# A graph layer with eight experts: the first two lots of tokens picked by one-hot products, and the parts without edges made in two PSUM banks

## The chip, the core and the metric

The kernel runs on one core of a Trainium2 chip. The metric is the device time of one execution in microseconds (us); the kernel before has a median of 1637.05 us over 5 runs (1624.28 to 1647.42). The engines are TensorE (PE, matrix products), VectorE (DVE), ScalarE (ACT), GpSimd (POOL, which here does nothing but issue indirect transfers) and SyncE (SP, which issues plain transfers). Each engine works through its own list of instructions in order and waits for the others by semaphores.

## The reference, cut to what matters

3125 nodes with 256 features, 100,000 edges sorted by their target node:

```python
xn = _layernorm(x, axis=-1)
x = x + gnn(xn, src, dst) + mix(xn)          # 3125 x 256
x = x + ffn(_layernorm(x, axis=-1))          # 8 experts, the 2 best of each token

# gnn: maximum over the edges that end in a node, 0 for a node without edges
e = relu((xn[dst] - xn[src]) @ theta.T + theta_b + xn[src] @ phi.T + phi_b)
out = segment_max(e, dst)

# ffn: a token goes to the two experts with the best logits
h = gelu(xe[e] @ W1[e] + b1[e])              # 256 -> 1024
y = h @ W2[e] + b2[e]                        # 1024 -> 256
out = sum over the two of weight * y
```

`mix` is a linear attention without softmax; it comes down to one 256x256 matrix that every node is multiplied by.

## The kernel before

**Tiles and groups.** The nodes lie in 25 tiles of 128. Since the edge gather is the longest work, the tiles are cut into five groups by the edges that end in them: group 0 is tiles 17 to 24, group 1 tiles 10 to 16, group 2 tiles 4 to 9, group 3 tiles 1 to 3, group 4 tile 0. The edges are gathered in 727 steps of 128 rows (`gather`, L127 to L130), 134 for group 0, 151 for group 1, 185 for group 2, 158 and 99 for the others. Each gathered row is folded into a running maximum on DVE (`fold`, L411 to L415). Eight gathers fill one of five windows (`wide`, pool of 5); a window is stored to DRAM by SP (`s_d`) and is then free. The largest targets, the first 16 nodes, have too many edges for that, and get their maxima in another way (`first_maxima`, L1206 on): it turns rows of a table by products with the identity (L1238), makes masks on PE (L1256) and takes maxima on DVE (L1222). It borrows one of the five windows for the rows that it turns.

**Parts without edges.** `without_edges` (L454 to L464) makes for each tile what doesn't depend on its edges: one row of biases (L452), two products of 128x512 (L459), and x itself through the identity (L460), all added up in one PSUM bank of 512 columns; two copies on ACT (L463, L464) bring it back. A class `Early` (L1385) gives it the bank: the tile named `trf`, of which there is one. `mixers` starts the 25 parts in order of the groups, 3.5 ticks apart in group 0 and 4.25 after that.

**Tokens.** When a group's edges are folded, `group` (L1424) starts `token_tile` for each of its tiles: the node's maximum is put together, x is updated, normalized into `xn2(i)`, and the router's logits and the two best experts are found. `dispatch` (L1397) then waits for the tiles of half a group, and `slots` (L589) counts for each expert which token comes where.

**Lots.** A lot is one expert with one group, 24 of them with 256 places (groups 0 to 2) and 8 with 128 (group 3). There are two ways to bring the tokens of a lot together:
- Groups 0 and 1: `dispatch` scatters each tile's rows to their places in DRAM (`xs_d`, two indirect transfers per tile, 8 for each half of group 0), ACT's queue loads the rows of two lots at a time (`rows`, L807), and `turn` (L848) transposes them on PE.
- Groups 2 and 3, called on chip (`on_chip`, L796): `hots` (L815 to L826) compares, for each tile of the group, the place numbers with the place that each token has for this expert, which gives a one-hot matrix for each tile; `turn` (L837) multiplies tile by one-hot and adds up over the tiles. That needs no transfer.

Both leave the turned lot in `trf`, and `scaled` (L859) puts it on ACT into `xe` with the expert's scale. Then `Units.run` makes 8 steps of the first product (L730) with a gelu each (L732), and the second product (L754) of a lot lies between the steps of the next one. `Stream.go` (L895 to L964) leads this: it prepares lot u+1 during lot u (`between`, L941 to L945): in step 1 it makes the one-hots of lot u+1 if that lot is on chip, and otherwise, if u is even, loads the rows of the next pair of lots. If the next lot is not prepared, the branch at L916 does it one after the other: load or one-hots, 8 ticks, turn, 2 ticks, scale, 2 ticks.

**What sets the order.** The order of instructions on PE, DVE, ACT and SP is written out by the program itself. Generators (`start`, L1350) yield a number of ticks until their next piece is due, and `tick` (L1354) runs what is due; each indirect transfer that POOL issues is one tick. Counted from the yields: the parts start at tick 180; the last of them, of tile 0, starts at 276. The scatter of the first half of group 0 comes at 258 and moves the clock to 266, that of the second half at 279 and moves it to 287. The ranks of the second half are known at 261. Group 0's lots are added to the list at 287. Lot 0 begins at 297, after load, turn and scale; lot 1 at 302, lot 2 at 317. `first_maxima` begins at 287 and its first transposes (L1238) stand at 293.

Of the kernel before, what the change touches and what calls it, by code (L numbers as in the profile page):

```python
# [19 lines left out]
P = 128  # L20
# [49 lines left out]
SPILL = 128  # L70
APART_3 = 32
# [9 lines left out]
def gps_layer(ctx: ExitStack, tc: tile.TileContext, x, src, dst, thetaT, phiT, biases, wq, wkvT,  # L81
# [507 lines left out]
    def slots(ro, ps, g, half, i0, i1, pick, taken, chosen=None):  # L589
# [38 lines left out]
        if chosen is not None:  # L628
            nc.vector.scalar_tensor_tensor(chosen[:, i0 - first:i1 - first, :], rank, 1.0, took, op0=OP.add, op1=OP.mult)
            clock["chosen", g, half] = True  # L630
            yield 1
# [29 lines left out]
        if chosen is not None:  # L661
            return
# [46 lines left out]
    class Units:  # L709
# [12 lines left out]
        def run(self, e, w1t, xe, w2t, done, between, parts, part):  # L722


            n = parts * part
            hT = []
            for f in range(FC):
                hp = self.ps.tile([P, ROWS], F32, name="hp")
                for c in range(2):
                    nc.tensor.matmul(hp[:, 0:n], w1t[:, c, f, :], xe[:, c, 0:n], start=(c == 0), stop=(c == 1))  # L730
                hT.append(self.hidden())
                nc.scalar.activation(hT[f][:, 0:n], hp[:, 0:n], AF.Gelu, bias=sm[:, 4 + f, e:e + 1])  # L732
                on_pe(n / P * 0.43)
# [33 lines left out]
    class Stream:  # L767


        def __init__(self, wts, act, ps):  # L770
            self.wts, self.act, self.ps = wts, act, ps
            self.lots, self.through, self.open = [], set(), True
            self.held = {}
            self.chosen = {}
            self.parts = []
            self.plan()
# [19 lines left out]
        def on_chip(self, u):  # L796
            return u < len(self.lots) and self.lots[u][0] >= G - 3
# [9 lines left out]
        def rows(self, v):  # L807
            if 2 * v < len(self.lots) and ("xs", v) not in self.held and not self.on_chip(2 * v):
                xs = self.held["xs", v] = self.at(v % 2)
                asked.append((self.lots[2 * v][0], move(nc.scalar, xs.rearrange("p (k s) d -> p k s d", k=2), self.two(v))))  # L810
                for g, put in sent:
                    if g > asked[-1][0]:
                        apart_in_rows(asked[-1][1], put)

        def hots(self, u):  # L815

            if self.on_chip(u) and ("hot", u) not in self.held:
                g, e = self.lots[u]
                n, nt = CAPS[g], GROUPS[g][1] - GROUPS[g][0]
                if g == G - 3:  # L820
                    flat = xn_hi[:, 7:13, :].rearrange("p s d -> p (s d)")
                else:
                    flat = xn_lo[:, 6:9, :].rearrange("p s d -> p (s d)")[:, u % 2 * nt * n:(u % 2 + 1) * nt * n]
                hot = self.held["hot", u] = flat.rearrange("p (i n) -> p i n", n=n)
                for i in range(nt):
                    nc.vector.tensor_scalar(hot[:, i, :], place_of[g], self.chosen[g][:, i, e:e + 1], None, op0=OP.is_equal)  # L826

        def turn(self, u):
            if ("hot", u) in self.held and ("tr", u) not in self.held:
# [12 lines left out]
                on_pe(1.5 if more is None else 6.1)  # L842
# [52 lines left out]
        def go(self):  # L895
# [5 lines left out]
            while True:  # L901
                if u == len(self.lots):
# [12 lines left out]
                    nc.scalar.activation(table, eps, AF.Gelu)  # L915
                if ("xe", u) not in self.held:  # L916
                    self.rows(u // 2)
# [467 lines left out]
    class Early:  # L1385

        def tile(self, shape, dt, name):
            return at_hand["ffp"].tile([P, 2, ROWS], dt, name="trf", bufs=1).rearrange("p c n -> p (c n)")
# [8 lines left out]
    def dispatch(g, half, i0, i1, top, top_i, taken):  # L1397
# [13 lines left out]
        yield from slots(ro, mm, g, half, i0, i1, made[0], taken)  # L1411
# [12 lines left out]
    def group(g):  # L1424
# [11 lines left out]
        if g >= G - 3 and g < G - 1:  # L1436
# [37 lines left out]
        if g < G - 2:  # L1474
            yield 5 if g < G - 3 else 0.5
            at_hand["ffn"].add(g)
# [163 lines left out]
    def mixers():  # L1640
# [195 lines left out]
```

## Time and profile before

| | us |
|---|---|
| median of 5 runs | 1637.05 |
| the profiled execution: its time, its span | 1623.73, 1621.9 |
| PE busy; weight load | 981.3; 736.7 |
| DVE busy | 794.9 |
| ACT busy | 331.9 |
| POOL busy | 837.1 |
| last gather of group 0's, group 1's, group 2's edges ends | 299.5, 584.1, 977.2 |
| last gather of all edges ends | 1448.1 |
| first gelu of group 0's, group 1's, group 2's lots | 597.4, 843.7, 1147.5 |

Mean granted TensorE clock: 0.788. In the rows of a timeline the columns are the start and the duration in us, engine, line, operation, output and input with partitions and elements, the number of merged instructions, and in brackets the idle time of the engine before it with what ended it. "issue" means that nothing seen in the profile was waited for, "remote" that what was waited for is not seen. The end of a matrix product is modelled, so a product can be done later than its row says. In the table of stretches the columns are the stretch, its length, and the busy time and number of instructions of PE, the weight load, DVE, ACT and POOL, then the granted clock, the DMA engines' busy share and the GB/s.

### The profile page before, as it was taken

The numbers are of one execution on the slowest core, as the hardware profiler recorded it, in microseconds if no ns is written. First come the engines' busy times: TensorE is split into PE (matmuls) and PEld (weight loads), VectorE is DVE, ScalarE is ACT, GpSimd is POOL, SyncE is SP. The second block draws the span as 40 slices with busy tenths as digits, with TensorE's granted clock in tenths as the row PEclk, the third lists the DMA queues.
The fourth block names the chain that finished last, engine by engine and source line by source line (L and its number), as shares of the span: only waits on it lengthen the run. The fifth ranks groups of instructions, "written<-read, shape, count | busy, mean of one in ns | idle before, by whom it ended". The sixth has DMA issues, their size and how long they took to land.

```text
span 1621.9 us, 14777 instructions
## 1 busy us (share of the span) xinstructions
PE 981.3 (61%) x4461; PEld 736.7 (45%) x4461; DVE 794.9 (49%) x2543; ACT 331.9 (20%) x799; POOL 837.1 (52%) x868
## 2 busy tenths in 40 slices
PE   3505775823528437648656777624787747679657
PEld 3402332412315126537535666513575535569547
DVE  4546974745318315437246566337566524424423
ACT  2301222300103012213112222102211103123212
POOL 6274465566564754554645544654555473642341
PEclk7756997966758768769868888756899977979869
DMA  7442564658436545657546786435476744647453
GB/s 234 137 127 84 195 223 141 208 181 316 168 91 227 183 127 182 204 170 244 186 139 193 263 275 208 156 110 204 130 255 206 259 136 156 228 158 276 139 170 134
DMA packets 100263, 300.96 MB, mean 186 GB/s; under 512 B 20099, under 2 KB 43002, under 8 KB 89550
## 3 DMA queue, kind: packets, MB, share of 16 engines
q0 software_dynamic: 41824, 113.70, 23.5%
q1 hardware_dynamic: 29180, 109.58, 17.5%
q10 hardware_dynamic: 29170, 76.65, 14.4%
q8 instruction: 37, 0.61, 0.1%
q14 instruction: 52, 0.43, 0.1%
HBM read 181.72 MB, written 118.13 MB: 185 GB/s over the span
## 4 chain that ended last, share of the span: by engine, by line
PE 36%; another core or an unknown queue 31%; DVE 14%; issue 12%; ACT 4%; DMA 2%; POOL 0%; ACTq 0%; SPq 0%; DVEq 0%; POOLq 0%
PE hp L730 13%; PE yp L754 9%; DVE g L414 4%; PE trf L837 3%; PE v L1291 2%; ACT ring L732 2%; PE k L1291 1%; PE trf L459 1%; PE mm L1256 1%; PE dots_p L1314 1%; DVE xn_hi L1222 1%; DVE tiles L1199 1%; PE mm L507 1%; DVE hit L343 1%
## 5 line engine op out<-in xcount | busy, mean ns | idle before, releaser
L129 POOL DMA_INDIRECT g<-b_d,srcI x727 | 706.1, 971 | 529.6 <-issue 238.7
L414 DVE SCALAR_TENSOR_TENSOR g<-g,cut 128x256 f32<-128x256 f32 x722 | 348.4, 483 | 60.7 <-DMA g<-b_d,srcI 25.2
L732 ACT ACTIVATE ring<-hp,sm 128x256 f32<-128x256 f32 (+1 forms) x320 | 137.1, 432 | 584.2 <-remote 242.4
L1222 DVE CUSTOM_DVE_ANT_0 xn_hi<-bT,mm 128x512 bf16<-128x512 f32 (+1 forms) x224 | 140.5, 627 | 211.0 <-remote 84.7
L730 PE MATMUL hp<-xe,big 128*128 128x256 f32 (+1 forms) x736 | 182.5, 374 | 97.8 <-ACT ring L732 68.5
L754 PE MATMUL yp<-big,ring 128*128 128x256 f32 x608 | 178.8, 416 | 11.8 <-ACT ring L732 5.3
L730 PEld LDWEIGHTS hp<-xe,big 128*128 128x128 f32 x736 | 129.3, 203 | 123.7 <-ACT ring L732 74.0
L730 PE MATMUL hp<-xe,w 128*128 128x256 f32 (+1 forms) x448 | 120.3, 405 | 103.5 <-issue 51.6
L730 PEld LDWEIGHTS hp<-xe,w 128*128 128x128 f32 x448 | 87.8, 227 | 122.5 <-issue 56.0
L754 PEld LDWEIGHTS yp<-big,ring 128*128 128x128 f32 x608 | 122.0, 213 | 30.8 <-ACT ring L732 5.7
L754 PE MATMUL yp<-w,ring 128*128 128x256 f32 x368 | 101.6, 398 | 0.0
L129 POOL DMA_INDIRECT r<-s_d,end_i x25 | 23.9, 958 | 115.6 <-DMA s_d<-g 41.2
L754 PEld LDWEIGHTS yp<-w,ring 128*128 128x128 f32 x368 | 71.5, 202 | 10.8
L1256 PE MATMUL mm<-ident_h,absent 128*128 128x128 bf16 x400 | 43.0, 234 | 41.0 <-issue 23.6
L129 POOL DMA_INDIRECT g<-ys_d,from_i x42 | 39.9, 949 | 40.1 <-DVE g L1577 21.8
L1300 DVE TENSOR_REDUCE var<-big 128x16 f32<-128x1024 f32 x25 | 30.4, 1216 | 61.3 <-ACT big L1297 55.6
L452 PE MATMUL trf<-thirds,which_bias 74*128 74x512 bf16 x25 | 11.6, 464 | 78.7 <-ACT x_sb L464 57.3
L1256 PEld LDWEIGHTS <-absent 128*128 128x128 bf16 x400 | 31.1, 105 | 57.2 <-issue 29.1
L1291 PE MATMUL v<-wkv,xn_hi 128*128 128x512 f32 x56 | 31.1, 682 | 36.9 <-ACT big L1296 32.1
L511 DVE TENSOR_SCALAR none<-mm 128x1 f32<-128x1 f32 x25 | 3.8, 153 | 97.2 <-remote 46.8
L837 PE MATMUL trf<-xn_hi,xn_lo 128*128 128x256 f32 x192 | 46.3, 393 | 3.7 <-DVE g L414 3.7
L563 DVE MAX8 top<-mm 128x8 f32<-128x8 f32 x25 | 4.3, 171 | 85.3 <-remote 58.7
(327 smaller groups left out, 1400.5 us busy)
## 6 DMA issues: line engine op xcount, KB each, us to landing
s_d<-g SPq DMA_DIRECT2D x75, 1024.0 KB
big<-in_w ACTq DMA_DIRECT2D x44, 512.0 KB
w<-in_w ACTq DMA_DIRECT2D x32, 512.0 KB
s_d<-g SPq DMA_DIRECT2D x13, 896.0 KB
g<-b_d,srcI POOLq DMA_INDIRECT x727
big<-in_w ACTq DMA_DIRECT2D x4, 2048.0 KB
ys_d<-ys ACTq DMA_DIRECT2D x24, 256.0 KB
xs_d<-zero ACTq DMA_DIRECT2D x16, 256.0 KB
```

What stands on the lines that cost most here:

```text
L129: got = nc.gpsimd.indirect_dma_start(out=to, out_offset=None, in_=table, in_offset=row_index(index))
L343: nc.vector.tensor_scalar(hit, keys[i], node[:, i:i + 1], 0.0, op0=OP.is_ge, op1=OP.add, accum_out=upto[:, i:i + 1])
L414: nc.vector.scalar_tensor_tensor(g[:, j, :], last, cut[:, t:t + 1], g[:, j, :], op0=OP.add, op1=OP.max)
L459: nc.tensor.matmul(am, xnT(i, c), am_w[:, c, :], start=False, stop=False)
L730: nc.tensor.matmul(hp[:, 0:n], w1t[:, c, f, :], xe[:, c, 0:n], start=(c == 0), stop=(c == 1))
L732: nc.scalar.activation(hT[f][:, 0:n], hp[:, 0:n], AF.Gelu, bias=sm[:, 4 + f, e:e + 1])
L754: nc.tensor.matmul(yp[r][0:part, :], hT[q][:, r * part:(r + 1) * part], w2t[:, q, :], start=(q == 0), stop=(q == FC - 1 and self.whole))
L837: nc.tensor.matmul(tr[:, c, 0:CAPS[g]], xn2(i)[:, c * P:(c + 1) * P], hot[:, i - i0, :], start=(i == i0), stop=(i == i1 - 1 and more is No ...
L1222: nc.vector.tensor_tensor_reduce(unread[:, 0:n * P], bT[:, h, 0:n * P], mask_p[:, 0:n * P], 1.0, NEG, op0=OP.add, op1=OP.max, accum_out=mo ...
L1256: nc.tensor.matmul(mask_p[:, i * P:(i + 1) * P], absent[:, at:at + 1].to_broadcast([P, P]), ident_h, start=True, stop=True)
L1291: nc.tensor.matmul(to, xnT(i, c), wkv[:, c, k * INNER:(k + 1) * INNER], start=(c == 0), stop=(c == 1))
L1300: nc.vector.tensor_reduce(var, sq, AX.X, OP.add)
```

## The change

It has three parts.
- A constant `AT_FIRST = 2`: the first two lots of group 0 count as on chip. Their one-hots (8 tiles of 128x256) lie in the first eight of the 14 slots of `ring`, both lots' in the same place, and their place numbers are those of group 2. For that `slots` keeps the ranks of group 0 in `chosen`, as for the later groups. Group 0's lots are added as soon as both halves have their ranks, and `go` makes lots 0 and 1 ready one after the other before lot 0 begins: one-hots, 2.5 ticks, turn, 5.5 ticks, scale, 1 tick. The scatters of group 0 stay as they are.
- A set `sent` of the groups whose scatters have been issued: rows are loaded for a lot only when its group is in it.
- The parts without edges use the two tiles named `hp` in place of the one named `trf`, so `hp` is declared with 512 columns (it took a bank of its own before as well), and they all start 3.25 ticks apart. 3 ticks after the last, `clock["parts"]` is set, for which `go` waits.

```diff
+AT_FIRST = 2
...
-        if chosen is not None:
+        if g >= G - 3:
             return
...
-                hp = self.ps.tile([P, ROWS], F32, name="hp")
+                hp = self.ps.tile([P, 2 * ROWS], F32, name="hp")
...
         def on_chip(self, u):
-            return u < len(self.lots) and self.lots[u][0] >= G - 3
+            return u < len(self.lots) and (self.lots[u][0] >= G - 3 or u < AT_FIRST)
...
         def rows(self, v):
-            if 2 * v < len(self.lots) and ("xs", v) not in self.held and not self.on_chip(2 * v):
+            if 2 * v < len(self.lots) and ("xs", v) not in self.held and self.lots[2 * v][0] in self.sent and not self.on_chip(2 * v):
...
-                if g == G - 3:
+                if g < G - 3:
+                    flat = ring[:, 0:nt, :].rearrange("p s d -> p (s d)")
+                elif g == G - 3:
...
-                    nc.vector.tensor_scalar(hot[:, i, :], place_of[g], self.chosen[g][:, i, e:e + 1], None, op0=OP.is_equal)
+                    nc.vector.tensor_scalar(hot[:, i, :], place_of[max(g, G - 3)], self.chosen[g][:, i, e:e + 1], None, op0=OP.is_equal)
...
-                on_pe(1.5 if more is None else 6.1)
+                on_pe(1.5 if g == G - 2 else 6.5)
...
                     nc.scalar.activation(table, eps, AF.Gelu)
+                for k in range(AT_FIRST if u == 0 else 0):
+                    while "parts" not in clock:
+                        yield 0.5
+                    self.hots(k)
+                    yield 2.5
+                    self.turn(k)
+                    yield 5.5
+                    self.scaled(k)
+                    yield 1
                 if ("xe", u) not in self.held:
+                    while not self.on_chip(u) and self.lots[u][0] not in self.sent:
+                        yield 0.5
                     self.rows(u // 2)
...
         def tile(self, shape, dt, name):
-            return at_hand["ffp"].tile([P, 2, ROWS], dt, name="trf", bufs=1).rearrange("p c n -> p (c n)")
+            return at_hand["ffp"].tile([P, 2 * ROWS], dt, name="hp")
...
+        if g == 0:
+            while clock.get(("chosen", g), 0) < i1 - i0:
+                yield 0.5
+            at_hand["ffn"].add(g)
...
-            at_hand["ffn"].add(g)
+            at_hand["ffn"].sent.add(g)
+            if g:
+                at_hand["ffn"].add(g)
...
                 start(without_edges(Early(), i))
-                yield 3.5 if g == 0 else 4.25
+                yield 3.25
+        yield 3
+        clock["parts"] = True
```

More of the change, by code (lines that the diff above doesn't have):

```diff
@@ L628, in slots @@
         if chosen is not None:
+            clock["chosen", g] = clock.get(("chosen", g), 0) + nt
             nc.vector.scalar_tensor_tensor(chosen[:, i0 - first:i1 - first, :], rank, 1.0, took, op0=OP.add, op1=OP.mult)
@@ L774, in __init__ @@
             self.chosen = {}
+            self.sent = set()
             self.parts = []
@@ L1410, in dispatch @@
             return
-        yield from slots(ro, mm, g, half, i0, i1, made[0], taken)
+        yield from slots(ro, mm, g, half, i0, i1, made[0], taken, at_hand["ffn"].chosen.get(g))
         yield BEHIND_SLOTS[g]
@@ L1435, in group @@
         slices = slices_of(g)
-        if g >= G - 3 and g < G - 1:
+        if g == 0 or G - 3 <= g < G - 1:
             at_hand["ffn"].chosen[g] = ro.tile([P, i1 - i0, E], F32, name=f"chosen{g}")
```

## The prediction

> **What bounds the kernel now.** I read the page's busy table first, then the slices, then the chain of waits, then the timelines of PE, ACT and POOL around the place that the change touches, and last the price rows.
>
> From the page:
>
> ```profile
> PE 981.3 (61%) x4461; PEld 736.7 (45%) x4461; DVE 794.9 (49%) x2543; ACT 331.9 (20%) x799; POOL 837.1 (52%) x868
> PE 36%; another core or an unknown queue 31%; DVE 14%; issue 12%; ACT 4%; DMA 2%; POOL 0%; ACTq 0%; SPq 0%; DVEq 0%; POOLq 0%
> L129 POOL DMA_INDIRECT g<-b_d,srcI x727 | 706.1, 971 | 529.6 <-issue 238.7
> ```
>
> No engine is full. POOL issues one gather every 1.25 us (0.95 busy and 0.30 between), and each engine works through an order fixed by the planner, so the end is set by whoever makes POOL stop: its 530 us idle are waits for windows that DVE has not folded, and DVE is mostly behind PE. The 31% "unknown" is the important part. It is not another core: there is one. The timelines of PE, ACT and POOL show it where the last parts without edges are made:
>
> ```profile
> 533.37 0.38 PE L452 MATMUL trf<-thirds,which_bias 74*128 74x512 bf16 x1 [0.74 <-ACT x_sb L464]
> 541.78 0.58 PE L452 MATMUL trf<-thirds,which_bias 74*128 74x512 bf16 x1 [5.88 <-remote]
> 542.16 3.62 PE L459 MATMUL trf<-am_w,xn_lo 128*128 128x512 f32 x4
> 545.57 0.77 PE L460 MATMUL trf<-x_sb,ident 128*128 128x256 f32 x2
> 557.95 0.58 PE L452 MATMUL trf<-thirds,which_bias 74*128 74x512 bf16 x1 [11.60 <-ACT x_sb L464]
> 575.50 0.58 PE L452 MATMUL trf<-thirds,which_bias 74*128 74x512 bf16 x1 [12.70 <-ACT x_sb L464]
> 592.92 1.08 PE L848 MATMUL trf<-ident,xn_hi 128*128 128x128 f32 x4 [12.65 <-DMA xn_hi<-xs_d]
> ```
>
> ```profile
> 532.67 0.37 ACT L463 COPY xn_lo<-trf 128x256 f32<-128x256 f32 x1 [2.61 <-issue]
> 557.25 0.37 ACT L463 COPY xn_lo<-trf 128x256 f32<-128x256 f32 x1 [15.52 <-remote]
> 588.80 0.37 ACT L463 COPY xn_lo<-trf 128x256 f32<-128x256 f32 x1 [13.35 <-remote]
> 589.04 0.38 ACTq L121 DMA_DIRECT2D xn_hi<-xs_d  x1
> ```
>
> ```profile
> 583.15 0.95 POOL L129 DMA_INDIRECT g<-b_d,srcI  x1 [0.30 <-issue]
> 595.98 0.95 POOL L129 DMA_INDIRECT g<-b_d,srcI  x1 [11.88 <-PE mm L1238]
> 632.23 0.95 POOL L129 DMA_INDIRECT r<-s_d,end_i  x1 [18.82 <-DMA s_d<-g]
> ```
>
> Until 533 a part takes 3.26 us (526.85, 530.11, 533.37). Then the same five rows need 14 to 17 us: PE's part of 541.78 is over by its rows at 546.3, ACT is released at 557.25. PE's results reach the next engine late while POOL issues gathers without a break (517 to 584), and soon after POOL stops at 584.1 everything is prompt again. The one-hots of a later group show the same handoff: DVE's L826 waits 2.80, 4.58 and 3.15 us for a PE that by its rows is done, until POOL's last gather before its gap:
>
> ```profile
> 1136.14 0.35 DVE L826 TENSOR_SCALAR xn_hi<-place,chosen 128x256 f32<-128x256 int16 x1 [2.80 <-remote]
> 1141.08 0.35 DVE L826 TENSOR_SCALAR xn_hi<-place,chosen 128x256 f32<-128x256 int16 x1 [4.58 <-remote]
> 1144.58 1.14 DVE L826 TENSOR_SCALAR xn_hi<-place,chosen 128x256 f32<-128x256 int16 x4 [3.15 <-remote]
> ```
>
> ```profile
> 1139.68 0.95 POOL L129 DMA_INDIRECT g<-b_d,srcI  x1 [0.31 <-issue]
> ```
>
> I call such a time a late stretch. What causes it I don't know; a handoff between engines costs 3 to 15 us in it, not 0.1. So lot 0 starts at 595.5 not because its rows are late (the second scatter was issued by 556.5) but because ACT reaches the load at 589.0, behind the last part.
>
> **The Trainium skill against this row.** The page SBUF — State Buffer, section Who interferes with whom, says that PE and ACT never wait on anyone and that transfers never contend with a compute engine. The row 545.57 to 557.25 disagrees, whatever the mechanism; the measurement decides. By the page the new products would run calm and the sum would be that of the first rival, 1621 us.
>
> **The change part by part.** The order of instructions follows from the yields; one tick is one POOL issue.
>
> *Parts closer together, in two banks.* Starts at ticks 180 to 276 move to 180 to 258. The work is the same. In the calm stretch PE idles 0.74 us of each 3.26 us part waiting for ACT's copy; with two banks that idle goes: 25 x 0.74 = 18.5 us if all of it were on the path, 0 if DVE's token chain is (it is the chain from 491 to 514). About six parts run back to back on the path (516 to 533): I take 6 x 0.74 = 4 us of gain, bounds 0 and 18. Five parts (the last at ticks 266 to 276) move ahead of the second half's slots, into the stretch 485 to 530, where PE is the busiest engine, 39.68 us of 45:
>
> ```profile
> 485.00:530.00 45.00, 39.68 (x131) 23.08 (x132) 35.16 (x142) 15.84 (x43) 19.75 (x20) 0.82 0.58 210
> ```
>
> That is 5 x 2.5 (3.26 less the idle) = 12.5 us of PE earlier. In exchange they vanish from the late stretch 533 to 589, which they filled. Behind the waiting PE there stand the tokens' products L507, L549 and L560, and POOL's first scatter waited 4.5 us at 512.8 for exactly these; it will wait longer.
> A rule speaks against the second bank: TensorE: Matmul & The Clock Gate, section HAM oscillation — how this bites in real kernels, tells of PSUM double-buffering that gave no further gain once PE had a contiguous run. By it the gain is 0 and the sum 4 us higher.
>
> *One-hots of lots 0 and 1.* Added on DVE: 16 comparisons of 128x256 at 0.348 (median of the row L826) = 5.6 us. Added on PE: 2 lots x 2 halves x 8 tiles = 32 products, two records each, 64 x 0.216 = 13.8 us, from this piece of the chain (start, us, what):
>
> ```profile
> 1199.60 2.59 PE trf L837 x12
> ```
>
> Removed: 8 transposes (0.9 us) and one 512 KB load on ACT's queue. The 16 scatters of group 0 all stay on POOL, for the other six lots. One more DVE row of 128x32 for each half's ranks (0.18 us) lies among the slots' rows. The Gelu table load (1.28 us on ACT, today at 589.5) comes 26 ticks earlier, behind the last shares and before nothing that changes the table: 0, or 1.3 us if ACT is what PE waits for there. ACT's scaling stays (1.02 a lot). Both lots' one-hots lie in the same eight slots of the ring, so DVE's second set waits for PE's first products, eight handoffs, the very row shown above; behind them on DVE stand the folds that free POOL's windows. Calm, this chain is 2.8 + 6.9 + 1.0, twice = 21 us; in a late stretch (8 handoffs x 3 to 4.6 us more, from the row L826) 24 to 37 us more, until POOL stops.
>
> *The load wait moves, it doesn't go.* Lot 0 and lot 1 no longer wait for the rows (589.04 issued, 592.92 used: 3.9 us). But lot 0's step 1 now takes the branch for a lot made on chip (lot 1), and lot 1 is odd, so nobody asks for the rows of lots 2 and 3 until lot 1 has ended: load, turn and scaling take 12 ticks there, as they did before lot 0. Lot 0 comes at tick 287 (after the scatter's jump) in place of 297, lot 1 ends near 305, and lot 2 starts at 317, where it starts today. From there on the two programs have the same order. Cost and gain of the load: 0, bounds -3.9 and +3.9.
>
> *What stands before the first transposes of first_maxima (L1238).* These free the window that POOL waits 11.88 us for. They stay at tick 293. Today four late parts (4 x 2.5 us of PE) and lot 0's transposes stand before them; after the change 13.8 us of products, all of lot 0's first half (32 records x 0.216 = 6.9) and two steps of lot 1 (16 x 0.216 = 3.5). That is 24.2 against 10.9: 13.3 us more PE work before the instruction that restarts POOL.
>
> **The sum**, made against the profiled execution (span 1621.9, its time 1623.73, which is 13.3 under the median 1637.05). L1238 runs at 593.8 today. All calm: 530 + 12.5 (moved parts) + 21 (one-hot chain) + 6.9 + 3.5 + 1 (half of L1238) = 575, 19 us earlier. All late until POOL has run out of windows: 589 + 12.5 + 6.9 + 1 (lot 1's products and scaling) + 6.9 + 3.5 + 1 = 621, 27 us later. The stretch has been late for every run of POOL of this length, but the five moved parts delay POOL's run too and part of the chain gets done in it; I take the point nearer to the late end, +13, less the 4 us of the second bank, and 1 us less since lot 0 is then over: **+8 us**. The next POOL stop (18.82 at 632, for the folds' store) passes it on, because the folds stand behind L1222, which stands behind L1238; nothing later has slack that I can name. 1623.7 + 8 = 1632 for a profiled execution, 1637 + 8 = **1645** for the median.
>
> **The rivals.**
> *Faster: the late stretch shrinks.* With no part left after tick 261, PE is done before the stretch begins, and the one-hot chain runs calm. For it: PE was prompt for 15 us after POOL's start at 517. Against it: the chain has more handoffs than the parts had. L1238 comes 19 us earlier, POOL's 11.88 us wait goes: -12 to -19, with the rest of the second bank's 18 at most -33; I price it at -16: 1621.
> *Slower: the chain sticks.* One mechanism: DVE's second set of one-hots waits for PE in the late stretch, with folds queued behind, so POOL stops for L1238 until 621: +27, and +13 more if the tokens' products of 485 to 530 pay for the moved parts as well: 1664 to 1677. It decides as soon as L1238 comes after 610 (16 us later, 1%).
> *It does nothing.* Lot 2 stands where it stood; if the shifts are covered, 1637, give or take 5.
>
> **Chances.** Forecast (+1 to +16) 0.38; nothing or a small gain 0.18; slower 0.30; faster 0.14. Taking 1% as about what a measurement of this kernel can tell (16 us; the five runs span 1624 to 1647), the edge of the faster case and of the small gains gives faster 0.18, same 0.48, slower 0.34. The likeliest case alone spans 1638 to 1653; the range to leave out 2 in 10 reaches into both sides: 1615 to 1674.
>
> **What would show it.** PE: L452 rows end before about 545 and alternate without the 0.74 idle; 32 records of L837 twice before the first L730. DVE: 16 rows of L826, the second eight with "remote" or PE waits. POOL: the wait ended by L1238 near 596 is longer than 11.88 (forecast about 20) and restarts near 606. A wait for the load stands before lot 2 and none before lot 0. It is wrong if L1238 comes before 590 (first rival), if POOL's wait there exceeds 35 us (second), or if the time from lot 2 to the end changes by more than 10 us, since there the programs are the same.

## The result, and the profile after

The changed kernel takes 1642.87 us (median of 37 runs, 1617.36 to 1661.32). The kernel before, run beside it, takes 1626.39 (63 runs, 1611.44 to 1648.51). The ratio is 1.0064, 95% interval 1.0043 to 1.0085, which is about 10 us. It is less than the ratio of the medians (1.0101), because the comparison leaves disturbed runs out. The profiled execution of the changed kernel has a span of 1632.3 us, against 1621.9.

Lines behind the diff's first insertions have moved in the changed kernel: its first transposes of `first_maxima` are L1254, the one-hot comparisons L831, their products L842, the scaling L864, the parts without edges L453 to L465, the first product L732, the transposes of loaded rows L853, the fold L415, the gather L130, the scatter L137. L1238, the transposes before, is now a maximum on DVE.

From the page of the changed kernel, the busy table, the chain and the gathers:

```profile
PE 999.8 (61%) x4517; PEld 752.5 (46%) x4517; DVE 799.9 (49%) x2561; ACT 333.1 (20%) x802; POOL 836.0 (51%) x868
PE 34%; another core or an unknown queue 31%; DVE 14%; issue 11%; POOL 4%; ACT 4%; DMA 1%; ACTq 0%; POOLq 0%; SPq 0%; DVEq 0%
L130 POOL DMA_INDIRECT g<-b_d,srcI x727 | 705.4, 970 | 539.7 <-issue 236.7
```

PE has 18.5 us more work, DVE 5.0, and nothing else has changed in kind: the chain still has its 31% without a known cause, and POOL's gathers wait 10 us longer (539.7 against 529.6). The place of the change, on PE, from its timeline:

```profile
527.08 0.59 PE L461 MATMUL hp<-x_sb,ident 128*128 128x256 f32 x2
532.68 5.64 PE L842 MATMUL trf<-ring,xn_hi 128*128 128x256 f32 x14 [5.00 <-DVE ring L831]
539.02 4.15 PE L842 MATMUL trf<-ring,xn_hi 128*128 128x256 f32 x18 [0.70 <-remote]
578.18 8.82 PE L842 MATMUL trf<-ring,xn_hi 128*128 128x256 f32 x32 [35.01 <-ACT xe L864]
586.84 7.09 PE L732 MATMUL hp<-xe,w 128*128 128x256 f32 x32
598.95 0.60 PE L1254 MATMUL mm<-ident,g 128*128 128x128 f32 x4
625.41 1.12 PE L853 MATMUL trf<-ident,xn_hi 128*128 128x128 f32 x4 [3.17 <-DMA xn_hi<-xs_d]
```

The same stretch on DVE, ACT and POOL:

```profile
531.30 2.32 DVE L831 TENSOR_SCALAR ring<-place,chosen 128x256 f32<-128x256 int16 x8
575.45 0.35 DVE L831 TENSOR_SCALAR ring<-place,chosen 128x256 f32<-128x256 int16 x1 [29.66 <-remote]
```

```profile
534.08 0.37 ACT L464 COPY xn_lo<-hp 128x256 f32<-128x256 f32 x1 [6.95 <-remote]
577.11 1.02 ACT L864 ACTIVATE xe<-trf,sm 128x256 f32<-128x256 f32 x2 [42.38 <-remote]
```

```profile
570.91 0.95 POOL L130 DMA_INDIRECT g<-b_d,srcI  x1 [0.30 <-issue]
586.46 0.95 POOL L130 DMA_INDIRECT g<-b_d,srcI  x1 [14.60 <-DVE g L415]
605.59 0.94 POOL L130 DMA_INDIRECT g<-b_d,srcI  x1 [2.96 <-remote]
628.02 0.95 POOL L130 DMA_INDIRECT r<-s_d,end_i  x1 [13.97 <-DMA s_d<-g]
```

The parts end on PE at 527.7; before, the last one began at 575.5. Lot 0's products are over at 543 by their rows; ACT's scaling of them starts at 577.1, DVE's second set of one-hots at 575.4, and lot 1's products at 578.2. POOL's last gather before its stop ends at 571.9, so these three come 3.6 to 6.3 us after POOL has stopped, and DVE's folds, which stand behind the second one-hots, are what POOL stops for. The first transposes come at 598.9; in the kernel before they stood here:

```profile
593.79 1.91 PE L1238 MATMUL mm<-ident,g 128*128 128x128 f32 x8
```

Two profiles say little by themselves. The second experiment below has the order of the kernel before until lot 16, and there the same transposes came 9.6 us earlier:

```profile
584.17 1.91 PE L1238 MATMUL mm<-ident,g 128*128 128x128 f32 x8
```

So a difference of 10 us between two profiles at one place is not a finding; the ratios decide, and the rows are read for place and releaser. Some of this scatter goes when the place is counted from POOL's first scatter of group 0. Its rows in the kernel before, in that second execution, in the changed kernel and in the third experiment (the parts alone) are:

```profile
517.25 1.02 POOL L136 DMA_INDIRECT xs_d<-xn_hi,slot_i  x1 [4.50 <-issue]
504.23 1.01 POOL L136 DMA_INDIRECT xs_d<-xn_hi,slot_i  x1 [8.11 <-issue]
514.56 1.24 POOL L137 DMA_INDIRECT xs_d<-xn_hi,slot_i  x1 [9.48 <-issue]
513.50 1.01 POOL L136 DMA_INDIRECT xs_d<-xn_hi,slot_i  x1 [8.52 <-issue]
```

From there to the first transposes it is 76.5 and 79.9 us with the old order, 84.4 in the changed kernel (84.6 in the first experiment, which has the same order there), and 48.9 with the parts alone (53.8 with one bank).

### The profile page after: what moved, and what is told of

Read it like the earlier page. It is cut to its first block, busy times and chain, and to the rows that moved or that the text cites. A ratio compares the mean times of both kernels' runs of the same rounds, so it can differ in the third digit from the quotient of the medians.

```text
span 1632.3 us, 14915 instructions
## 1 busy us (share of the span) xinstructions
PE 999.8 (61%) x4517; PEld 752.5 (46%) x4517; DVE 799.9 (49%) x2561; ACT 333.1 (20%) x802; POOL 836.0 (51%) x868
## 4 chain that ended last, share of the span: by engine, by line
PE 34%; another core or an unknown queue 31%; DVE 14%; issue 11%; POOL 4%; ACT 4%; DMA 1%; ACTq 0%; POOLq 0%; SPq 0%; DVEq 0%
PE hp L732 11%; PE yp L756 9%; DVE g L415 4%; POOL g L130 4%; PE hp L460 3%; PE trf L842 2%; PE v L1307 2%; ACT ring L734 1%; DVE xn_hi L1238 1%; PE mm L1272 1%; PE k L1307 1%; PE mm L508 1%; DMA g<-b_d,srcI 1%; PE hp L461 1%
## 5 line engine op out<-in xcount | busy, mean ns | idle before, releaser
L130 POOL DMA_INDIRECT g<-b_d,srcI x727 | 705.4, 970 | 539.7 <-issue 236.7
L415 DVE SCALAR_TENSOR_TENSOR g<-g,cut 128x256 f32<-128x256 f32 x722 | 347.9, 482 | 53.9 <-DMA g<-b_d,srcI 14.2
L732 PE MATMUL hp<-xe,big 128*128 128x256 f32 (+1 forms) x736 | 187.0, 382 | 105.6 <-issue 54.8
L1238 DVE CUSTOM_DVE_ANT_0 xn_hi<-bT,mm 128x512 bf16<-128x512 f32 (+1 forms) x224 | 140.4, 627 | 220.9 <-remote 120.2
L732 PEld LDWEIGHTS hp<-xe,big 128*128 128x128 f32 x736 | 133.4, 209 | 134.5 <-issue 61.0
L732 PE MATMUL hp<-xe,w 128*128 128x256 f32 (+1 forms) x448 | 114.9, 391 | 88.6 <-ACT xe L864 39.4
L732 PEld LDWEIGHTS hp<-xe,w 128*128 128x128 f32 x448 | 86.2, 219 | 104.2 <-ACT xe L864 40.4
L130 POOL DMA_INDIRECT r<-s_d,end_i x25 | 23.7, 948 | 112.0 <-issue 61.7
L130 POOL DMA_INDIRECT g<-ys_d,from_i x42 | 40.0, 952 | 60.3 <-DVE g L1599 27.9
L1307 PE MATMUL v<-wkv,xn_hi 128*128 128x512 f32 x56 | 36.0, 777 | 36.0 <-ACT big L1312 23.4
L864 ACT ACTIVATE xe<-trf,sm 128x256 f32<-128x256 f32 (+1 forms) x64 | 30.8, 535 | 112.6 <-remote 87.6
L842 PE MATMUL trf<-xn_hi,xn_lo 128*128 128x256 f32 x192 | 47.3, 399 | 3.7 <-DVE g L415 3.7
L842 PE MATMUL trf<-ring,xn_hi 128*128 128x256 f32 x64 | 18.6, 458 | 40.7 <-ACT xe L864 35.0
L842 PEld LDWEIGHTS trf<-xn_hi,xn_lo 128*128 128x128 f32 x192 | 37.5, 199 | 9.6 <-DVE g L415 4.0
```

Source lines behind the costliest of these rows:

```text
L130: got = nc.gpsimd.indirect_dma_start(out=to, out_offset=None, in_=table, in_offset=row_index(index))
L415: nc.vector.scalar_tensor_tensor(g[:, j, :], last, cut[:, t:t + 1], g[:, j, :], op0=OP.add, op1=OP.max)
L842: nc.tensor.matmul(tr[:, c, 0:CAPS[g]], xn2(i)[:, c * P:(c + 1) * P], hot[:, i - i0, :], start=(i == i0), stop=(i == i1 - 1 and more is No ...
L864: nc.scalar.activation(xe[:, c, 0:n], self.held["tr", u][:, c, 0:n], AF.Identity, bias=sm[:, 2 + c, e:e + 1], scale=sm[:, c, e:e + 1])
L1238: nc.vector.tensor_tensor_reduce(unread[:, 0:n * P], bT[:, h, 0:n * P], mask_p[:, 0:n * P], 1.0, NEG, op0=OP.add, op1=OP.max, accum_out=mo ...
L1307: nc.tensor.matmul(to, xnT(i, c), wkv[:, c, k * INNER:(k + 1) * INNER], start=(c == 0), stop=(c == 1))
```

## The experiments

Twelve kernels, in three series of four, each series on a chip of its own with runs of the kernel before on the same chip. In the first two series that kernel has medians of 1630.29 and 1629.77 us. On the chip of the third series the same kernel took 1159.82, so the four ratios of that series stand for another condition, which the last section shows. In brackets behind a ratio stands its 95% interval. On the first two chips the ratio of the medians of all runs can differ from the ratio given by up to 0.006; where that matters, it is said.

**Group 2's cost put back.** The diff changes the planner's cost of a product turn for all groups: before, a turn without spilled rows (rows of a lot that come through DRAM and are added at L840) was planned at 1.5 us and one with them at 6.1. Lot 17 has no spilled rows (before's L840 has 56 records, eight for each of seven lots), so 1.5 becomes 6.5 for it.

```diff
-                on_pe(1.5 if g == G - 2 else 6.5)
+                on_pe(6.5 if g < G - 3 else 1.5 if more is None else 6.1)
```

> The changed kernel, with the planner's cost of a product turn put back for group 2: 6.5 for the two lots of group 0, then as before (1.5 for a turn without spilled rows, 6.1 with them). The changed line gives 6.5 us to lot 17, which has no spilled rows and had 1.5 before, and 0.4 more to the other lots of group 2; counted from the yields, lot 18 begins 5 ticks later for it, lot 23 8 ticks and lot 31 16 ticks. Here they all begin where they began before, and lots 0 to 15 stay as in the changed kernel. Theory A (the loss stands behind lots 16 to 23, by this cost): lots 0 to 15 keep their gain of about 5 to 9 us and the end comes 5 to 10 us earlier than before, ratio 0.994 to 0.998. Theory B (the one on record: the loss stands at lots 0 and 1 and the first transposes of first_maxima, and is passed on): nothing changes against the changed kernel, ratio 1.004 to 1.009. Theory C (any shift of the order moves the time by some tenths of a per cent, without direction): ratio anywhere from 0.993 to 1.010, not in step with the next run.

Measured: 1.0115 (1.0052 to 1.0179). No gain. Theory A, that the changed kernel loses its time by this line, is wrong; B fits, with a size on the upper side. C, by which any shift of the order moves the time, isn't ruled out.

**That cost alone**, in the kernel before.

```diff
-                on_pe(1.5 if more is None else 6.1)
+                on_pe(1.5 if g == G - 2 else 6.5)
```

> The kernel before, with that one line alone: each turn of group 2 is planned at 6.5 us, lot 17's too. Not one instruction is added or taken away; lots 17 to 31 move by 1 to 16 ticks in the order, everything up to lot 16 stays. Theory A: it is slower by what the changed kernel lost from lot 16 to the end in the two profiles, 10 to 18 us, ratio 1.006 to 1.011. Theory B: 1.000, give or take 0.002. Theory C: anything from 0.993 to 1.010.

Measured: 1.0065 (1.0013 to 1.0117). By the medians of all runs it is 1.0116. As A said here, and against B: moving lots 17 to 31 by 1 to 16 ticks costs time by itself. With the run before it this shows that the two costs don't add: if they did, taking the line out of the changed kernel would give 0.9999, and 1.0115 lies 0.0116 above that, give or take 0.0085. Why they don't add is not shown; C, the shift without direction, fits both runs.

**The parts alone.**

```diff
-                hp = self.ps.tile([P, ROWS], F32, name="hp")
+                hp = self.ps.tile([P, 2 * ROWS], F32, name="hp")
...
-            return at_hand["ffp"].tile([P, 2, ROWS], dt, name="trf", bufs=1).rearrange("p c n -> p (c n)")
+            return at_hand["ffp"].tile([P, 2 * ROWS], dt, name="hp")
...
-                yield 3.5 if g == 0 else 4.25
+                yield 3.25
```

> The kernel before, with the parts without edges alone changed: two banks in turn, 3.25 ticks apart, nothing made on chip for group 0, the cost as before. All lots begin at their old ticks. Theory A: ACT is free of the parts when the rows of lots 0 and 1 can be loaded, so lot 0 starts earlier, by up to the 9 us seen in the pair of profiles; POOL's wait for the first transposes of first_maxima shrinks; ratio 0.994 to 0.999. Theory B: the five moved parts cost 12.5 us of PE in 485 to 530 and 4 are won, four late parts (10 us of PE) no longer stand before these transposes: ratio 0.998 to 1.002. Theory C: as above.

Measured: 0.9876 (0.9802 to 0.9949), 20 us faster, more than any theory gave it, though the interval just reaches A's range. The size is less sure than the interval: there are six runs, and the medians of all runs (1620.15 and 1630.29) lie only 10 us apart. PE and POOL in the same stretch:

```profile
526.53 0.59 PE L460 MATMUL hp<-x_sb,ident 128*128 128x256 f32 x2
561.47 1.12 PE L848 MATMUL trf<-ident,xn_hi 128*128 128x128 f32 x4 [34.34 <-DMA xn_hi<-xs_d]
562.38 1.91 PE L1238 MATMUL mm<-ident,g 128*128 128x128 f32 x8
```

```profile
598.91 1.07 POOL L129 DMA_INDIRECT g<-b_d,srcI  x1 [8.63 <-DVE g L414]
616.43 0.94 POOL L129 DMA_INDIRECT r<-s_d,end_i  x1 [8.72 <-DMA s_d<-g]
```

With the last part done at 527, PE waits for one thing only, the rows of lots 0 and 1, which ACT can ask for at 557 as nothing else is in its way. The transposes come at 562.4, and POOL doesn't stop for them at all: its two stops up to 620 are 8.63 and 8.72 us, where the kernel before had 11.88 and 18.82.

**One bank, with the on-chip lots** (group 2's cost back, parts in `trf`).

```diff
-            return at_hand["ffp"].tile([P, 2 * ROWS], dt, name="hp")
+            return at_hand["ffp"].tile([P, 2, ROWS], dt, name="trf", bufs=1).rearrange("p c n -> p (c n)")
```

> The first of these four kernels (cost back), but the parts take the one bank named trf, as before, still 3.25 ticks (4.1 us) apart. It tells what the second bank is worth. On record: 4 us of gain, bounds 0 and 18, from a PE that idles 0.74 us of each 3.26 us part. If the second bank matters: 4 us over the first kernel, up to 18 (ratio to before higher by 0.0025 to 0.011). If only the place of the parts matters: the same as the first kernel within 0.002. Theories A and B expect 4 us; A holds 0 possible, since parts 4.1 us apart leave room for the wait.

Measured: 1.0120 (1.0047 to 1.0193), the same as with two banks (1.0115), give or take 0.010.

**One bank, parts alone.** The kernel before with only `yield 3.25`.

> The kernel before with its parts 3.25 ticks apart, but still in the one bank trf: the parts alone (0.9876) less the second bank. If the gain of the parts alone is the place (they are over before POOL's long stretch, so nobody waits there for ACT to empty the bank), this is the same as the parts alone within 0.004, and the first transposes of first_maxima come near 562 again. If it is the second bank, half or more of the 1.2% goes: 0.994 to 1.000. On record: the bank is worth 4 us, 0.0025.

Measured: 0.9920 (0.9856 to 0.9984); the transposes at 572.3. By these ratios most of the gain is the place of the parts; by the medians of all runs (1626.78 and 1629.77) it is only 3 us, so its size is open. The second bank is worth 0.0044, with an uncertainty of 0.010 (the two half-widths, 0.0073 and 0.0064, added as squares): the 4 us on record are possible, so is nothing.

**The parts alone, and products that nobody reads.**

```diff
+        def more_pe(self):
+            while clock["now"] < 269:
+                yield 0.5
+            for _ in range(2):
+                tr = self.ps.tile([P, 2, ROWS], F32, name="trf", bufs=1)
+                for c in range(2):
+                    for i in range(*GROUPS[0]):
+                        nc.tensor.matmul(tr[:, c, :], xn2(i)[:, c * P:(c + 1) * P], xn2(i), ...)
+                yield 9
```

> The parts alone (two banks, 3.25 ticks), and at tick 269 two times 16 products of 128x256 of group 0's rows, as many as the one-hot products of lots 0 and 1, written to trf and read by nobody; no one-hots, nothing else moved in the order. On record the on-chip part costs because PE has 13.3 us more work in front of the first transposes of first_maxima. Theory W (the work): these transposes and POOL's restart come about 14 us later than with the parts alone, ratio 0.994 to 1.000. Theory H (the handoffs: in the changed kernel the second set of one-hots waits 29.66 us for products that by their rows ended at 538, ACT's scaling 42.38, PE 35.01, until POOL has stopped): products without a handoff go into PE's idle time, 34.34 us before 561 with the parts alone; ratio 0.985 to 0.992.

Measured: 0.9989 (0.9948 to 1.0030). That is 0.0113 more than the parts alone, or 18 us, give or take 14. By the number, theory W is right. The rows say that it is right for another reason (this execution lies 0.8% over its kernel's median, so they are read for place only):

```profile
528.90 6.42 PE L902 MATMUL trf<-xn_hi 128*128 128x256 f32 x29
541.24 0.59 PE L902 MATMUL trf<-xn_hi 128*128 128x256 f32 x1 [2.25 <-issue]
584.92 9.32 PE L902 MATMUL trf<-xn_hi 128*128 128x256 f32 x32 [43.09 <-remote]
597.30 1.04 PE L1250 MATMUL mm<-ident,g 128*128 128x128 f32 x8
```

```profile
598.61 0.94 POOL L129 DMA_INDIRECT g<-b_d,srcI  x1 [19.18 <-PE mm L1250]
```

The first 16 products are issued by 541.2, and the second 16, which go to the same tile `trf`, start 43 us later, when POOL has stopped (its last gather ended at 579.4). The kernel was meant to have no handoff, but it has one: as nobody else uses `trf` in between, the second set can by the program only wait for the end of the first, though the row says just "remote". PE has idle time in plenty for 13.8 us of work; it is the wait between the two sets that holds the transposes back to 597. The second set holds back something else too: the rows of lots 0 and 1 are loaded over places that it reads (tiles 18 to 21), so ACT asks for them at 592.98, where the parts alone did at 557.20, and PE waits 2.60 us more for them ahead of the transposes.

**Places of its own for the second set of one-hots** (group 2's cost back).

```diff
                     flat = ring[:, 0:nt, :].rearrange("p s d -> p (s d)")
+                    if u == 1:
+                        more = self.act.tile([P, 2, ROWS], F32, name="over", bufs=1)
+                        flat = [ring[:, nt + i, :] if i < 6 else more[:, i - 6, :] for i in range(nt)]
```

> The changed kernel with group 2's cost put back, and the one-hots of lot 1 in eight places of their own (six more slots of ring, two in a tile that is free then), so that DVE makes them without waiting for PE, and the folds behind them go on. DVE's wait of about 30 us before the second set is gone in every theory. H1 (the stuck one-hots hold up the folds, POOL stops for these at 572, and that is the loss): POOL goes on past 572, the first transposes of first_maxima come 10 to 30 us earlier, ratio 0.988 to 1.000. H2 (any handoff in this stretch sticks until POOL stops: lot 1's products still need ACT to have emptied trf of lot 0, and the transposes stand behind them on PE): POOL now stops only when its windows are full, at about 584, everything behind it follows then, the transposes near 605 to 612, ratio 1.010 to 1.020. W: as the kernel it is made from, 1.006 to 1.012.

Measured: 1.0076 (1.0034 to 1.0117), within the spread of its three relatives, as W said. DVE makes the second set at 535 without a wait. On PE and POOL (this execution is the longest of its twelve, 0.6% over the median, so again for place only):

```profile
525.66 8.78 PE L845 MATMUL trf<-ring,xn_hi 128*128 128x256 f32 x32 [2.56 <-DVE slot_f L667]
592.24 5.30 PE L845 MATMUL trf<-ring,xn_hi 128*128 128x256 f32 x12 [57.79 <-ACT xe L867]
613.79 0.60 PE L1257 MATMUL mm<-ident,g 128*128 128x128 f32 x4
```

```profile
616.83 0.95 POOL L130 DMA_INDIRECT g<-b_d,srcI  x1 [29.22 <-PE mm L1257]
```

This is H2's sequence, and H1 falls by the ratio: with the folds free POOL goes on, but for 2.70 us, until 587.6, everything sticks so much longer (PE 57.79 in place of 35.01), and one long stop for the transposes replaces the stop for the folds. The price is below H2's range, though its interval reaches into it; it doesn't tell H2 from W.

**Rows of lots 2 and 3 asked for in lot 1** (group 2's cost back).

```diff
-                elif u % 2 == 0:
+                elif u % 2 == 0 or u + 1 == AT_FIRST:
```

> The changed kernel with group 2's cost put back, and lot 1 asks in its step 1 for the rows of lots 2 and 3, which the changed kernel asks for only when lot 1 is over: counted from the yields, lot 2 begins at tick 306 in place of 318, lot 7 at 382 in place of 389, lot 8 as before. If the lots of group 0 bound what follows: lot 2's first gelu comes 10 to 15 us earlier than 632 and so does the end, ratio 0.997 to 1.005. If, as on record, POOL's stops set the pace and the lots run beside them: the end stays, ratio 1.006 to 1.013 as the kernel it is made from (1.0115).

Measured: 1.0062 (1.0024 to 1.0099). Lot 2 came at 613.4 in place of 632.1. Against the kernel it is made from the ratio is 0.0053 lower, give or take 0.0074: it doesn't tell whether the lots matter at all here. The two ratios are also from two chips, and by the medians of all runs this one is 1.0022.

**The third chip.** Its four kernels were made for the late stretch, and it wasn't there: with the on-chip lots PE waits 5.28 us before lot 1's products, where the changed kernel waited 35.01, and POOL makes no stop between 300 and 520. Memsets between the gathers, once with the on-chip lots (group 2's cost back) and once with the parts alone:

```diff
         behind([got])
+        if 258 <= clock["now"] <= 300:
+            behind([nc.gpsimd.memset(pause, 0.0)])
```

> The changed kernel with group 2's cost put back, and behind each of POOL's gathers of ticks 258 to 300 a memset of 128x64 on POOL into a tile that nobody reads, so that the gathers come about 1.4 to 1.5 us apart in place of 1.25. Nothing else moves. Theory L (PE's and ACT's results come late because POOL issues gathers back to back: in the profile of the parts alone the handoffs of 557 to 566 were prompt, and there the gathers stood 1.41 us apart): the second one-hots no longer wait 30 us, ACT's scaling 42, POOL doesn't stop for folds at 572; the first transposes of first_maxima come at 565 to 585; ratio 0.988 to 1.000 although POOL has some 8 us more to do. If the spacing has nothing to do with it: the same waits, and 5 to 8 us more: 1.010 to 1.018.

> The parts alone (two banks, 3.25 ticks), with the same memsets between the gathers of ticks 258 to 300. With the parts alone POOL did not stop before 582, so the handoffs have less to win: theory L gives 0.982 to 0.990 (the late gelu of 585, which waited 21 us, comes earlier), the other 0.990 to 0.996 (8 us of POOL on its path).

Measured: 1.0021 (1.0001 to 1.0041) and 1.0013 (0.9998 to 1.0027). The edit did not do what it was for: a memset takes 0.17 us and fits into the 0.30 us that lie between two gathers, which stay 1.27 us apart. So the expectations are not tested. As a comparison of the on-chip lots with the parts alone it still counts: they differ by 0.0008, 1 us, give or take 0.0025.

**The first transposes ahead of the one-hots** (group 2's cost back).

```diff
-                    while "parts" not in clock:
+                    while "turned" not in clock:
...
+                if h:
+                    clock["turned"] = True
                 yield 2
                 nc.scalar.copy(bT[:, h, 0:n * P], turned_p[:, 0:n * P])
```

> The changed kernel with group 2's cost put back, but lots 0 and 1 are made ready only when the first transposes of first_maxima have been given to PE, so that no product of the one-hots stands before them. All of it is kept, only its place: counted from the yields, lot 0 begins at about tick 315, lot 2 at 344 in place of 318, lot 15 at 551 in place of 520, still before the lots of group 2 at 583. Theory W (on record: the on-chip part costs by what it puts in front of these transposes): they come at 545 to 575, POOL doesn't stop for them, ratio 0.987 to 0.998 though the lots are 25 to 30 ticks later. If the on-chip part costs by its work and handoffs wherever they stand, or by late lots: 1.005 to 1.020.

Measured: 1.0024 (1.0008 to 1.0039). So late, the rows of tile 17 have been overwritten by the maxima of `first_maxima`, which share their place, so lot 1 is made from other numbers; the instructions are the same. Lot 2 came at 497.2, where the spaced on-chip kernel had 461.5, lot 15 at 765.7 against 725.2, and the end did not move (spans 1160.4 and 1164.3): on this chip the lots of the first two groups are not on the path. What the expectation asked, the late stretch without products ahead of the transposes, stays untested.

**Parts and the cost line.** The parts alone and `on_pe(1.5 if g == G - 2 else 6.5)`.

> The parts alone with the planner's cost line of the change, 6.5 for every turn of group 2: a second measurement of this line. Alone on the kernel before it gave 1.0065 (1.0013 to 1.0117), while putting it back in the changed kernel gave no gain. If it costs some 10 us wherever it stands: 0.9876 + 0.0065 = 0.994, within 0.990 to 0.998. If its effect depends on the state in which group 2 is reached: 0.985 to 0.990 or above 1.000.

Measured: 1.0030 (1.0016 to 1.0043). The parts with memsets, whose lots of group 2 stand where they stood, had 1.0013 beside the same runs; so here the line costs 0.0017, 2 us, give or take 0.0020, if the memsets are free. Neither expectation was written for this chip; by size it is nearer to a line that costs what it meets than to 10 us everywhere.

## Why the prediction was right, point by point

The total held (10 us slower, forecast 8), and the likeliest case was the right one. But two of its terms were wrong by more than the total, with opposite signs, so that the total came out is in good part luck.

*The late stretch.* Right as an observation: it is there again after the change and in the kernels of the first two series shown above. Wrong in its condition: I tied it to POOL issuing gathers without a break. On the third chip POOL does just that and the same handoffs are prompt.

*Parts closer together.* The step that failed inside the sum is the 12.5 us of cost for the moved parts and the 4 us of gain. Measured alone the parts gain 20 us (8 to 32; 10 by the medians of all runs), and by the run with one bank 13 of these come without the second bank. The cost is not seen. PE's busy time in 485 to 530 is 33.16 us, and the 39.68 that I built on was 34.16 in the second execution of the old order. POOL's first scatter waits longer, as I wrote (9.48 against 4.50 us), but it comes at 514.56, between the 504.23 and 517.25 of the two executions with the old order. By ACT's copies all 25 parts now take 143 us, from 391.2 to 534.7, in place of 200. The gain lies where I had counted only 10 us of PE: in the late stretch the last parts follow each other 14.0 to 17.6 us apart on ACT, so taking four of them from before the transposes is worth more than their 2.5 us of work each.

What I weighed there from the Trainium skill (TensorE: Matmul & The Clock Gate, section HAM oscillation — how this bites in real kernels: no further gain from PSUM double-buffering) is a measurement of one other kernel, not a rule. These runs neither bear it out nor refute it: 0.0044 with an uncertainty of 0.010.

*One-hots of lots 0 and 1.* DVE's work was priced well, 4.6 us in rows against 5.6; PE's was too low, 18.6 (5.64 + 4.15 + 8.82) against 13.8. The handoffs were near in sum but not in form: I priced eight at 3 to 4.6 us, 24 to 37 together. The trace shows one between the sets, of 29.66 us on DVE, 42.38 on ACT and 35.01 on PE at the same time, and it ends when POOL stops. It is the mechanism of my second rival, "the chain sticks". The stuck folds make POOL stop at 572 in place of 584, and the chain goes on from there; with places of its own for the second set POOL ran on to 587.6, and so did the wait. My 27 us for it were counted against the kernel before, where the transposes came only 5 us later; against the parts alone they came 37 us later, so the gain of the parts hid most of it. Four kernels with the on-chip lots and the old cost have 1.0062 to 1.0120, the parts alone 0.9876: the on-chip lots cost 30 to 40 us on these chips, give or take some 15, and by the medians of the first series 25.

*The load wait moves.* Right: PE waits 3.17 us for the rows before lot 2. That "from there on the two programs have the same order" is wrong: I read the changed `on_pe` as a price of the new lots and missed that it plans group 2 anew. Alone it costs 0.65% (0.13 to 1.17). In the changed kernel putting it back gains nothing.

*The transposes.* I forecast 13.3 us more work before L1238 and a wait of about 20 us that ends near 606. The two stops that took its place are 14.60 and 2.96, and the second ends at 605.6. But the larger one is for DVE's folds, so the place was right and its reason in part not. That the transposes pay for what stands before them is shown by the parts alone (562, no stop) and the products alone (597, a stop of 19.18); that they pay for PE's *work* is not: a handoff between two sets of products explains it, and no run on the first two chips has the work without the handoff. On the third chip, where the handoff is short (5.28 us), the same work costs 1 us, give or take 3; that speaks for the handoff, though there POOL doesn't stop for the transposes anyway. A second PSUM tile for lot 1's products on one of the first two chips would decide it; it was not tried.

*What would prove it wrong.* Of the three signs two stayed away: the transposes came at 598.9, not before 590, and POOL's wait for them was far under 35. The third appeared: from lot 2's first gelu to the end it took 17 us more (1003.0 against 985.6), where I had held the programs to be the same. The cost line is the difference there, and its interval alone (2 to 19 us) would allow it. But two executions don't show it: with the line put back in the changed kernel the same stretch still took 996.8 us, and with the parts alone, where the order behind lot 2 is that of the kernel before, 997.8. So most of the 17 us may lie in one short execution of the kernel before.

What stays open: how much of the change's 0.64% is the cost line, how large the gain of the parts is, and whether the changed kernel as a whole is slower on a chip of the third kind, where its on-chip lots cost 1 us, give or take 3.

The best kernel of the study is the parts alone, 0.9876, where handoffs are late; on the third chip, with memsets, it has 1.0013.

## What to carry to other kernels

Price a chain by its handoffs before its work, above all two users of one PSUM tile: on two of the three chips they held PE for 35 to 58 us with PE idle. When a diff edits a line of a planner's cost, look up every caller of that line, and measure the line alone. And run the kernel before several times, on more than one chip, before building on a stretch of one trace: what looked like a property of the program was one of where or when it ran. A sum of parts can come out right by two errors that cancel; measure the parts of a change one by one.

## What the runs showed of the hardware

The same program took 1630 us on two chips and 1160 on a third. Each chip was measured in one session only, so "chip" may stand for something else that differed between the sessions. The page of the parts alone, on one of the first two, has these groups:

```profile
L129 POOL DMA_INDIRECT g<-b_d,srcI x727 | 705.9, 971 | 534.2 <-issue 236.6 <-DVE g L414 140.0 <-DMA s_d<-g 44.5
L732 ACT ACTIVATE ring<-hp,sm 128x256 f32<-128x256 f32 (+1 forms) x320 | 136.7, 431 | 590.0 <-remote 278.2 <-PE hp L730 242.6 <-issue 31.9
```

and on the third chip, from the kernel with the parts and the cost line:

```profile
L129 POOL DMA_INDIRECT g<-b_d,srcI x727 | 712.4, 980 | 229.2 <-issue 197.8 <-DMA g<-b_d,srcI 10.7 <-DVE g L414 9.7
L732 ACT ACTIVATE ring<-hp,sm 128x256 f32<-128x256 f32 (+1 forms) x320 | 137.7, 431 | 346.7 <-PE hp L730 342.2 <-DMA big<-in_w 4.0
```

A gather takes as long (971 and 980 ns), a gelu too (431), but ACT's 278 us of waiting for something unseen are gone, and 305 us of POOL's idle time too: the 727 gathers run nearly without a break (0.30 us between two would make 218 of the 229.2 us), and the last ends at 1056.3 us of 1160.8. The granted clock is 0.787 on the one and 0.893 on the other, which can't be it alone: the spans differ by 456 us (1616.8 and 1160.8), PE's busy time by 73 (967.7 and 894.4). On the third chip ACT follows PE at once while POOL gathers every 1.25 us (start, us):

```profile
436.40 0.47 ACT L732 ACTIVATE ring<-hp,sm 128x256 f32<-128x256 f32 x1 [0.39 <-PE hp L730]
437.26 0.47 ACT L732 ACTIVATE ring<-hp,sm 128x256 f32<-128x256 f32 x1 [0.39 <-PE hp L730]
```

```profile
436.34 0.95 POOL L129 DMA_INDIRECT g<-b_d,srcI  x1 [0.30 <-DMA g<-b_d,srcI]
437.59 0.95 POOL L129 DMA_INDIRECT g<-b_d,srcI  x1 [0.30 <-issue]
```

The handoff of the on-chip lots itself, in the kernel with memsets on the third chip:

```profile
401.40 8.95 PE L845 MATMUL trf<-ring,xn_hi 128*128 128x256 f32 x32 [5.28 <-DVE ring L834]
```

So gathers back to back don't make handoffs late by themselves; something in the condition of the first two chips does, and these runs don't show what. There, not only the handoffs but PE's own issue slowed down: in the kernel with the unread products three of them came one at a time, at 536.26, 538.41 and 541.24, with nothing to wait for. What the Trainium skill says (SBUF — State Buffer, section Who interferes with whom: PE and ACT never wait on anyone) is said of the engines' ports to SBUF. Ahead of the result I read it as a statement on handoffs, and that was too much: a wait of 35.01 us on one chip and 5.28 on another is not shown to be a wait at a port, so these rows neither contradict the section nor bear it out.
